# A four-direction scan block in fp32: all four directions of an image in one step of eight lines, ordered by a list scheduler

## The chip, the core and the metric

The kernel runs on one core of a Trainium2 chip; everything is fp32. The metric is the device time of one launch in microseconds (us), the median of several. The core's engines run side by side, each through its own queue in order: TensorE (PE; its weight loads are listed as PEld), VectorE (DVE), ScalarE (ACT), GpSimd (POOL) and SyncE (SP), which here issues the transfers (DMAs). Where an engine needs another's result, its instruction waits at the head of its queue.

## What is computed

The input is x[4, 128, 96, 96]. It is group-normalised, read as four sequences of 9216 positions per image (row by row, the same backwards, column by column, the same backwards), each sequence goes through the block below, and the four results are put back in place, mixed by a 1x1 convolution and added to x:

```python
t = grouped1x1(x, in_proj_w, in_proj_b, 4); u, gate = t[:, :256], t[:, 256:]
u = conv5_depthwise(silu(u), dw_w)
s = ssm_in_w @ u                                  # 32 channels
a = 0.999 + 0.0009 * sigmoid(ssm_delta_w @ u + .) # decay of the scan
bb, cc = tanh(ssm_b_w @ u + .), tanh(ssm_c_w @ u + .)
h[n] = a[n] * h[n-1] + bb[n] * s[n]               # along the sequence
u = u + ssm_out_w @ (cc * h + ssm_d * s)
y = out_proj_w @ grouped1x1(u * sigmoid(gate), mix_w, mix_b, 4) + .
out = x + fuse_w @ concat(y of the four directions)
```

The 256 channels of u stand in two halves of 128 partitions, j = 0 and j = 1. mix, out_proj and fuse are folded into one weight, w_fin, per direction.

## The kernel before

**Tiling.** An image is done in two phases, first the two vertical directions, then the two horizontal ones; the eight phases make up the launch. A phase has six steps of 16 lines. The positions of a step are kept by their residue modulo 4 (R = 4, order of the residues 1, 0, 3, 2), 384 positions each. One pair n (192 in all, 24 a phase) is one residue of one step for both directions, s = 0 and s = 1; the backward direction works from the other end of the image. So in the first three steps of a phase (here: fresh pairs) both directions meet new lines, and their silu tiles and gates are computed and also stored to DRAM; in the last three (mirrored pairs) each meets the lines that the other has had, and silu tiles and gates come back from DRAM, read backwards.

**A pair, with the names of the order table.** `F0..F3`/`SIL` (L245, L647): input projection and silu, fresh only; sixteen 32x32 products. `C0, C1` (L245, tile `band`): most of the convolution of half j = 0 as products with band matrices of 128 rows; the taps that reach over the band's edge come by `L` (tile `less`, 64-row products, for two residues of four) or by `E` (L766, one DVE operation on a tile `edge` that a DMA has shifted over the partitions). `T0` (L783, ACT) and `T1..T4` (L785, DVE): the five taps of half j = 1. `P0a..P1b` (L245, `u,main`): projections to delta, b, s, c, 32 rows for each direction, so s, b and the scan stand on 64 partitions. `TM, SC, CT` (L801, L809, L812), `SS` (L830), `DEC, BS` (L823, L826, POOL): the scan's inputs. `SCAN0, SCAN1` (L843, DVE): once for four residues, in two halves of 64 partitions x 768. `CH, ADD, CP` (L849, L853, L856, POOL). `UND` (L862, ACT copies u into PSUM), `S` (L866, ssm_out added there), `G`/`TH` (L872, L878: gate, fresh only), `GAT` (L919, DVE). `W` (L245, `u,w_fin`): four products of 32 columns each for a direction and half. `YS` (L932, L930) and `ACC` (L972, POOL): added to `acc`, the whole image in SBUF. While an image is done, the group statistics of the next are taken from chunks of it (`XC` loads 128x768 into `xs`, two `BN_STATS`, L518).

**Order.** Five tables are written out: `PLAN` (the operations of a pair's slot for four kinds of slot), `LAGS` (how many pairs an operation lags), `BANKS`, `START` and `END` (first eight slots and last six, operation by operation). PSUM has eight banks, handed out by `rent`. Every transfer takes one of eight semaphores in turn, so an issue also waits until the transfer eight places before it has landed; in the built program these are DMAHW0 to DMAHW7, in both kernels.

All small products are issued through one helper (L245), so its line stands for F, C, L, P and W; they are told apart by their tiles:

```python
def mm(o, col, lhsT, rhs, start, stop):      # L243
    r = slice(32 * col, 32 * col + 32)
    nc.tensor.matmul(o[r, : rhs.shape[-1]], lhsT, rhs, start=start, stop=stop,
                     skip_group_check=True)
def conv_less(n, to):                        # L, for two residues of four
    for g in range(4):
        for s in range(2):
            r = less_rows(s, p)              # 64 rows
            mm(bank(to[s]), g, less[p][r, g, :], columns(step, sil[s][r, g, :], k), False, True)
def result(n, s, j, to):                     # W
    for c in range(4):
        mm(bank(to), c, w_fin[:, units[2 * n + s]["dir"], j, 32 * c : 32 * c + 32],
           us[n][:, s, j, :], first, not first)
```

An fp32 product shows as two records in the trace, so "x8" in a row of it is four products.

Of the kernel before, what the change touches and what calls it, by code (L numbers as in the profile page):

```python
# [1 line left out]

# [40 lines left out]
F32 = mybir.dt.float32  # L43
# [14 lines left out]
LN = 16  # L58
NS = HH // LN
N = LN * WW // R  # L60
M = WW // R
UB = 8
NP = NS * R

PLAN = {
    "front": """
        T1 F1 F3 CP YS1 TM F2 F0 DEC P1b T2 P0b W01 AU0 SIL1 SIL3 SIL0 W00 SC BS T3 T4 SIL2 ZERO
        UND1 SCAN0 UND0 AU1 YS0 G00 C0 C1 S11 CT SS S00 ACC0 ACC1 S10 G01 SCAN1 S01 CH BN G10 E
        AFTER TH0 G11 L W10 W11 GAT0 TH1 UC P0a GAT1 ADD TH2 P1a T0 TH3
    """,  # L70
    "both": """
        YS1 T1 F2 F0 TM CP SCAN1 T2 F3 F1 C0 C1 SIL1 SIL0 P0b SIL2 T3 DEC SIL3 ZERO P1b L S11
        S10 T4 CT CH G10 SS G00 UC ADD TH2 W01 UND1 E AFTER W00 SC G01 ACC1 BN S01 YS0 ACC0 S00
        UND0 G11 AU1 TH0 GAT1 AU0 W10 W11 TH1 SCAN0 BS GAT0 P0a P1a T0 TH3
    """,
    "gate": """
        P0b YS1 CP AU1 P1b ACC1 T1 TM T2 AU0 UND1 C1 DEC CT C0 SC W00 L T3 SS T4 UND0 W01 BS S11
        E AFTER SCAN1 S10 G00 CH UC YS0 S00 G01 G11 TH0 BN S01 ACC0 G10 SCAN0 TH1 GAT1 W11 W10
        ADD P1a T0 P0a TH3 GAT0 TH2
    """,  # L80
    "none": """
        C0 T1 C1 TH1 P0b L W00 CP T2 P1b YS1 W01 TH0 TM ACC1 TH3 UND0 CH UC S01 E AFTER UND1 SC
        DEC T3 YS0 S00 G10 G11 AU0 S10 S11 T4 SCAN1 CT G01 BS BN G00 ADD SCAN0 GAT1 ACC0 AU1 TH2
        T0 P0a W10 SS W11 P1a GAT0
    """,
}
LAGS = {
# [6 lines left out]
}  # L94
BANKS = {
# [87 lines left out]
def conv_preact_kernel(  # L183
# [52 lines left out]
    def bank(i):  # L236
        return psum[:, i, :]
# [1065 lines left out]
```

## Time and profile before

| | before |
|---|---|
| median of two runs | 1777.9 us (1777.7 to 1778.11) |
| profiled execution: its span | 1770.6 us |
| instructions: PE, DVE, ACT, POOL | 22584, 1541, 2571, 1500 |
| mean granted TensorE clock | 0.994 (0.83 in the first 30 us, 0.93 from 30 to 100 us) |
| moved by DMA | 377.69 MB, 213 GB/s |
| launch to first input projection | 24.0 us |

The profile's first part gives each engine's busy time and its share of the span; products overlap on PE, so its busy share says only that something was in flight. A row of the groups has line, engine, operation, tiles, shape and count, then busy time, mean duration of one in ns, then the idle time ahead of it and what ended it. A row of the timeline has start and length in us. The median of the runs lies 7.3 us above the span of the profiled execution.

### The profile page before, as it was taken

Reading aid. Unit: us, or ns where it says so; the run is one execution under the profiler, and the core shown is the slowest. Engines: PE = TensorE matmul, PEld = TensorE weight load, DVE = VectorE, ACT = ScalarE, POOL = GpSimd, SP = SyncE. Lnnn points to the kernel's source line nnn. Section 1 sums busy time; section 2 is a strip of 40 time slices with the busy share of each in tenths; the row PEclk is TensorE's granted clock in tenths of the full one; section 3 lists DMA queues with packets and bytes.
Section 4 is the critical chain, followed back from the end, with each engine's and each line's share of the span. In section 5 each row is a group of like instructions: output and inputs, shape, how many; then the busy total and the mean of one; then the engine's idle time right before and its main releaser. Section 6 shows DMA issues by size and latency. Waiting matters only on the chain.

```text
span 1770.6 us, 54587 instructions
## 1 busy us (share of the span) xinstructions
PE 1747.7 (99%) x22584; PEld 638.7 (36%) x22584; DVE 1516.8 (86%) x1541; ACT 1486.1 (84%) x2571; POOL 1394.0 (79%) x1500
## 2 busy tenths in 40 slices
PE   6999999999999999999999999999999999999999
PEld 3333333333333333333333333333333333333333
DVE  4899988888788988988888988898888878888898
ACT  5788888888888888888888888888888888888875
POOL 4488888878778888788877888878777788887776
PEclk7999999999999999999999999999999999999999
DMA  7776676665987678564798657755589755656654
GB/s 229 180 238 232 180 227 187 201 204 175 295 261 235 209 209 241 182 204 165 218 293 264 231 188 227 223 179 198 165 257 278 250 193 181 209 159 198 215 190 165
DMA packets 183767, 377.69 MB, mean 213 GB/s; under 512 B 16736, under 2 KB 147040, under 8 KB 183520
## 3 DMA queue, kind: packets, MB, share of 16 engines
q1 hardware_dynamic: 183376, 374.16, 67.4%
q8 instruction: 178, 2.92, 0.7%
q14 instruction: 69, 0.57, 0.1%
q10 hardware_dynamic: 144, 0.04, 0.0%
HBM read 222.96 MB, written 151.18 MB: 211 GB/s over the span
## 4 chain that ended last, share of the span: by engine, by line
PE 91%; DMA 3%; ACT 2%; issue 1%; SPq 1%; DVE 1%; POOL 0%; ACTq 0%; POOLq 0%; DVEq 0%
PE psum L245 78%; PE psum L866 10%; PE psum L872 4%; DMA acc<-in_xr 2%; DMA out<-acc 1%; ACT gate L878 1%; POOL acc L972 0%; SPq L713 0%; DMA x_in<-in_xs 0%; ACT psum L862 0%; DVE u L919 0%; ACT sil L647 0%; DMA edge<-edge 0%; ACT u L748 0%; ACT t L812 0%
## 5 line engine op out<-in xcount | busy, mean ns | idle before, releaser
L785 DVE SCALAR_TENSOR_TENSOR psum<-sil,small,psum 128x768 f32<-128x768 f32 x576 | 588.1, 1022 | 56.1 <-ACT psum L783 38.1
L245 PE MATMUL psum<-u,w_fin 128*32 128x384 f32 x6144 | 580.0, 490 | 0.9
L245 PE MATMUL psum<-u,main 128*32 128x384 f32 x6144 | 562.2, 488 | 1.8 <-ACT gate L878 0.7
L972 POOL TENSOR_TENSOR acc<-ys,acc 128x384 f32<-128x384 f32 x365 | 422.1, 1165 | 155.2 <-ACT ys L932 76.8
L919 DVE SCALAR_TENSOR_TENSOR u<-gate,psum 128x768 f32<-128x768 f32 x376 | 346.0, 951 | 97.1 <-PE psum L866 69.9
L245 PEld LDWEIGHTS psum<-u,main 128*32 128x32 f32 x6144 | 186.6, 109 | 325.9 <-issue 216.0
L245 PEld LDWEIGHTS psum<-u,w_fin 128*32 128x32 f32 x6144 | 175.3, 109 | 342.8 <-issue 241.9
L862 ACT COPY psum<-u 128x768 f32<-128x768 f32 x352 | 278.1, 800 | 23.6 <-DVE u L766 8.4
L849 POOL TENSOR_TENSOR t<-t,t 64x384 f32<-64x384 f32 x192 | 235.1, 1225 | 68.4 <-DVE t L843 32.2
L245 PE MATMUL psum<-sil,band 128*32 128x384 f32 x3072 | 287.6, 490 | 1.1 <-ACT ys L932 1.1
L866 PE MATMUL psum<-t,main 32*128 32x384 f32 x1536 | 257.4, 530 | 1.3 <-ACT psum L862 1.3
L853 POOL TENSOR_TENSOR t<-t,t 64x384 f32<-64x384 f32 x192 | 236.9, 1234 | 7.6
L878 ACT ACTIVATE gate<-psum,bnorm 128x384 f32<-128x384 f32 x384 | 211.7, 577 | 33.4 <-PE psum L872 15.6
L826 POOL TENSOR_TENSOR t<-t,tm 64x384 f32<-64x384 f32 x191 | 196.0, 1026 | 51.1 <-ACT t L809 39.0
L823 POOL TENSOR_SCALAR t<-tm 64x384 f32<-64x384 f32 x191 | 179.7, 941 | 51.3 <-ACT tm L801 36.2
L647 ACT ACTIVATE sil<-psum,bnorm 128x385 f32<-128x385 f32 x384 | 200.4, 581 | 22.4 <-PE psum L245 21.8
L785 DVE SCALAR_TENSOR_TENSOR u<-sil,small,psum 128x768 f32<-128x768 f32 x192 | 194.7, 1014 | 18.2
L783 ACT ACTIVATE psum<-sil,small 128x768 f32<-128x768 f32 x192 | 173.7, 905 | 36.2 <-DVE u L919 31.5
L872 PE MATMUL psum<-x_in,wn 32*128 32x384 f32 x768 | 187.9, 516 | 0.2
L801 ACT ACTIVATE tm<-psum,small 128x384 f32<-128x384 f32 x192 | 112.5, 586 | 59.5 <-PE psum L245 57.2
L245 PEld LDWEIGHTS psum<-sil,band 128*32 128x32 f32 x3072 | 97.2, 110 | 152.4 <-issue 102.1
L932 ACT COPY ys<-psum 128x384 f32<-128x384 f32 x278 | 133.1, 479 | 21.3 <-POOL acc L972 10.9
(84 smaller groups left out, 1442.3 us busy)
## 6 DMA issues: line engine op xcount, KB each, us to landing
sil<-sil SPq DMA_DIRECT2D x128, 770.0 KB, 7.1
kept<-gate SPq DMA_DIRECT2D x80, 768.0 KB, 4.4
gate<-kept SPq DMA_DIRECT2D x76, 768.0 KB, 5.7
edge<-edge SPq DMA_DIRECT2D x96, 384.0 KB, 5.9
x_in<-in_xs SPq DMA_DIRECT2D x192, 96.2 KB, 3.5
edge<-sil SPq DMA_DIRECT2D x96, 192.5 KB, 3.9
acc<-in_xr SPq DMA_DIRECT2D x47, 384.0 KB, 7.8
out<-acc SPq DMA_DIRECT2D x44, 384.0 KB, 3.8
```

Of the source, the lines that this page charges most:

```text
L245: nc.tensor.matmul(o[r, : rhs.shape[-1]], lhsT, rhs, start=start, stop=stop, skip_group_check=True)
L647: nc.scalar.activation(sils[step][:, j, s, g, :], bank(frm)[:, : N + 1], AF.Silu, bias=bn[:, 1:2] if j else bn[:, 4 + g : 5 + g],)
L785: nc.vector.scalar_tensor_tensor(u_of(n)[:, :, 1, :] if k == K - 1 else part, src, w_tap[:, k : k + 1], part, ALU.mult, ALU.add,)
L826: engine.tensor_mul(scan_of(n)[0:64, pair_of(n)["p"], :], tbs[n][0:64, :], tms[n][0:64, :])
L849: engine.tensor_mul(ta[0:64, p, :], tbs[n][64:P, :], ta[64:P, p, :])
L853: engine.tensor_add(z, scans[n // R][0:64, pair_of(n)["p"], :], z)
L862: nc.scalar.copy(two(to), us[n][:, s])
L866: nc.tensor.matmul(bank(to)[:, :N], w_so[r, bass.ts(j, P)], tbs[n][r, :], start=not seeded(n), stop=True, skip_group_check=True)
L872: nc.tensor.matmul(bank(to)[:, :N], stats[pair_of(n)["b"]][0][r, s, :], x_in[s][r, q, off : off + N], start=True, stop=True)
L878: nc.scalar.activation(gates[n % 2][:, s, j, :], bank(frm)[:, :N], AF.Tanh, bias=bn[:, 2 + j : 3 + j], scale=0.5,)
L919: nc.vector.scalar_tensor_tensor(v, g, 1.0, two(frm), ALU.add, ALU.mult)
L972: nc.gpsimd.tensor_add(to, y, part)
```

## The change

The kernel is written anew around another split of the same work.

- **Split.** The four directions of an image are done together. A step has eight lines (12 steps an image, 6 fresh and 6 mirrored), a residue has 192 positions in each direction, and one n (192 in all) is one residue for four directions; operations that took 2 x 384 columns take 4 x 192. Projections to delta, b, s, c are done for two n at once (`P`, 384 columns, four directions on 4 x 32 partitions), so `DEC`, `BS`, `SS`, `CH`, `ADD` take 128 partitions and are half as many, and `SCAN` is one operation of 128 x 768 for a step. `CP` and the ACT copy `UC` are gone.
- **Edges.** `L` is gone. The taps that the band does not cover come from the tile `edge`: residues 0 and 3 need one, residues 1 and 2 need two. Fresh: `E` for one, `EH` and `E` for two, all DVE. Mirrored, two taps: `ES` (ACT) and `EA`, `EB` (POOL, 128 x 768) make `pre`, and DVE adds it (`E`). The edge tile is filled by 32 transfers of 32 x 386 a fresh step (SBUF to SBUF) and 8 of 128 x 386 a mirrored one (from DRAM).
- **Results.** `W` runs 192 columns at a time, for two directions into one bank: eight products where there were four. `YS` covers two directions, `ACC` adds each by itself, 128 x 192, in pieces of 8 or of 2 adjoining columns.
- **Statistics.** `XC` loads one chunk of 128 x 384, into one buffer `xs`; 72 of them for 72 `BN_STATS`.
- **Order.** No tables: every operation is added to a `Plan` with its reads and writes, a cost and a rank, and a list scheduler goes through assumed time and gives each free engine its ready operation of lowest rank. It takes a transfer to land 2 us after its bytes have gone through at 330 GB/s, and knows nothing of the eight semaphores.

```diff
-LN = 16
+S4 = 4
+BL = 8
...
-PLAN = { ... }  LAGS = { ... }  BANKS = { ... }  END = """ ... """  START = """ ... """
+COST = {"F": 890, "G": 860, "S": 860, "C": 645, "PJ": 645, "W": 645, "turn": 113, ... "T": 1022, "GAT": 951, "SCAN": 2100, "ACC": 650, ... }
+RANK = {"F": -4.33, "SIL": 0.47, ... "BN": -1.47, "STAT": 0.44}
+                if e == "SP":
+                    dma_free = max(dma_free, now) + pick.bytes / 330.0
+                    heapq.heappush(events, (now + 60, tick, 0, pick))
+                    tick += 1
+                    heapq.heappush(events, (dma_free + 2000, tick, 1, pick))
...
-    def conv_less(n, to): ...
+                if fresh:
+                    for g in range(R):
+                        dma(f"LE{k0}_{e}_{h}_{i}_{g}", k0 + 2 * e - 1.2, ...
+                                to[32 * g : 32 * g + 32],
+                                sil[32 * blk : 32 * blk + 32, ti, 0, g, 2 * h : 2 * h + 2, :]), ...)
...
+            nc.vector.tensor_tensor_scan(
+                t, t, bsb.rearrange("p n r -> p (n r)"),
+                0.0 if st == 0 else hbuf[:, 1 - hs, N - 1, R - 1 : R], ALU.mult, ALU.add)
...
+                    for o in range(2):
+                        s = 2 * h + o
+                        for c in range(4):
+                            mm(bank(w[key][0])[:, o * N : o * N + N], c,
+                               w_fin[:, DIRS[s], j, 32 * c : 32 * c + 32], ubuf[:, j, s, sl, :],
+                               j == 0 and o == 0, j == 1 and o == 1)
...
+    def chunk(b, c, n):
+        dma(f"XC{b}_{c}", n - 1.5, lambda: nc.sync.dma_start(xs, xr[b, :, bass.ds(c * SC, SC)]),
+            P * SC * 4, reads=[("done", n - 3)], writes=["xs"])
+        add(f"BN{b}_{c}", "DVE", "BN", n + RANK["BN"],
+            lambda w: nc.vector.bn_stats(stats_of(b)[:, c, :], xs), reads=["xs"], writes=[("bn", b, c)])
...
-        start()
-        for t in range(HEAD, NPAIR - TAIL):
-            slot(t)
-        tail()
+        for _, op, w in seq:
```

Where instructions stand now, at three places. On PE in the fresh half, before (L866 is `S`, L872 is `G`, `band` is C, `less` is L):

```order
L866 MATMUL psum<-t_56_5947,main 128x384 x2
L872 MATMUL psum<-x_in_70,wn_4136 128x384
L866 MATMUL psum<-t_56_5947,main 128x384
L872 MATMUL psum<-x_in_70,wn_4136 128x384
L872 MATMUL psum<-x_in_71,wn_4136 128x384
L866 MATMUL psum<-t_56_5947,main 128x384
L872 MATMUL psum<-x_in_71,wn_4136 128x384
L245 MATMUL psum<-u_5763,w_fin 32x384 x8
L245 MATMUL psum<-u_6417,main 32x384 x16
L245 MATMUL psum<-sil_5425,band 32x384 x8
L245 MATMUL psum<-u_5868,w_fin 32x384 x4
L245 MATMUL psum<-sil_5425,less 32x384 x8
```

and now (L855 is `S`, L633 `G`, `x_f` F):

```order
L250 MATMUL psum<-u,main 32x384 x4
L250 MATMUL psum<-u,w_fin 32x192 x8
L855 MATMUL psum<-csb,main 128x384 x4
L250 MATMUL psum<-u,w_fin 32x192 x48
L855 MATMUL psum<-csb,main 128x384 x4
L250 MATMUL psum<-sil,band 32x2x192 x8
L633 MATMUL psum<-x_g,wn_323 128x384 x4
L250 MATMUL psum<-x_f,wn_323 32x386 x16
L250 MATMUL psum<-u,main 32x384 x20
```

The 64-row products are gone, `S` and `G` stand in sets of four products and no longer mixed, and `W` has twice the products. Counted over the whole order, runs of 128-row products (`C`, `P`, `W` between others) go from 357 to 329.

On DVE in a fresh step now (L725 is `E`, L741 `T`, L815 `SCAN`, L957 `BN_STATS`):

```order
L725 SCALAR_TENSOR_TENSOR u<-edge,small,psum 128x4x192
L741 SCALAR_TENSOR_TENSOR psum<-sil,small,psum 128x4x192 x2
L957 BN_STATS bn_682<-xs 128x6
L741 SCALAR_TENSOR_TENSOR psum<-sil,small,psum 128x4x192
L741 SCALAR_TENSOR_TENSOR u<-sil,small,psum 128x4x192
L725 SCALAR_TENSOR_TENSOR u<-edge,small,psum 128x4x192
L815 SCALAR_TENSOR_TENSOR h<-h,bs 128x768
L741 SCALAR_TENSOR_TENSOR psum<-sil,small,psum 128x4x192
L957 BN_STATS bn_682<-xs 128x6
```

A chunk's load is released by the `E` of three n before it (or by the chunk before, if that is later), and its `BN_STATS` stands close behind: in 38 of the 72 cases at most three operations lie between.

On SP in a fresh step now (L591 and L598 fill `edge`, L954 is the chunk's load, L660 stores gates, L557 the silu tile, L509 and L623 load x):

```order
L660 DMA gate_5_0_280<-gate 128x1536
L660 DMA gate_5_1_281<-gate 128x1536
L954 DMA xs<-in_xr 128x384
L591 DMA edge<-sil 32x386 x16
L954 DMA xs<-in_xr 128x384
L623 DMA x_g<-in_xg 128x768
L954 DMA xs<-in_xr 128x384
L591 DMA edge<-sil 32x386 x4
```

A fresh step now issues 51 transfers (32 edges, 8 silu, 4 gates, 4 chunks, 3 of x), and the launch 1724 where it issued 1037; several chunk loads stand right behind 8 to 16 edge loads.

More of the change, by code (lines that the diff above doesn't have):

```diff
@@ L388, in load @@
+        return one, two, three, four, five, six, seven, eight, nine
     def load(src, name, pool=wp, queue=nc.scalar):
@@ L487, in conv_preact_kernel @@
     nc.scalar.activation(b_fin, pb[:, 0:1], AF.Identity, bias=b_fuse)
+    nc.vector.tensor_scalar_mul(b_fin, b_fin, 0.5)
     prep.__exit__(None, None, None)
[L490 to L509 removed]
@@ L598, in conv_preact_kernel, with buf @@
-    opened = set()
-    def opens(key):
-        opened.add(key) if (first := key not in opened) else None
-        return first
-    sils, edges, us, scans, tbs, tms, yss, old_gates = {}, {}, {}, {}, {}, {}, {}, {}
-    qb, qc, qa, qs = (slice(MH * i, MH * (i + 1)) for i in range(4))
+    wk = ctx.enter_context(tc.tile_pool(name="work", bufs=1))
+    def buf(name, *shape):
+        return wk.tile([P, *shape], F32, tag=name, name=name)
+    sil = buf("sil", 2, 2, R, S4, N + 1)
+    ubuf = buf("u", 2, S4, UB, N)
```

1624 lines of the change are left out of this document (748 added, 876 removed), and 15 rows, old and new, of tables (COST, LAGS, MOVES).

## Prediction

> **What bounds the kernel now.** First the page: its shares, then the chain of waits.
>
> ```profile
> span 1770.6 us, 54587 instructions
> PE 1747.7 (99%) x22584; PEld 638.7 (36%) x22584; DVE 1516.8 (86%) x1541; ACT 1486.1 (84%) x2571; POOL 1394.0 (79%) x1500
> PE 91%; DMA 3%; ACT 2%; issue 1%; SPq 1%; DVE 1%; POOL 0%; ACTq 0%; POOLq 0%; DVEq 0%
> ```
>
> PE is in flight for 99% and carries 91% of the chain. Overlapping products make that share a poor measure of work, so next the timeline of PE, whose start-to-start distances are the price of each kind of set:
>
> ```profile
> 265.12 0.88 PE L245 MATMUL psum<-sil,less 64*32 64x384 f32 x16
> 265.93 1.50 PE L245 MATMUL psum<-u,w_fin 128*32 128x384 f32 x16
> 268.64 0.95 PE L245 MATMUL psum<-x_in,wn 32*32 32x385 f32 x32
> 269.52 1.50 PE L245 MATMUL psum<-u,main 128*32 128x384 f32 x16
> ...
> 609.76 0.59 PE L866 MATMUL psum<-t,main 32*128 32x384 f32 x2
> ...
> 611.58 1.50 PE L245 MATMUL psum<-u,w_fin 128*32 128x384 f32 x16
> ...
> 615.47 0.83 PE L245 MATMUL psum<-u,main 128*32 128x384 f32 x8
> 616.12 0.83 PE L245 MATMUL psum<-u,w_fin 128*32 128x384 f32 x8
> 616.76 0.83 PE L245 MATMUL psum<-u,main 128*32 128x384 f32 x8
> 617.41 0.83 PE L245 MATMUL psum<-u,w_fin 128*32 128x384 f32 x8
> 618.16 0.93 PE L866 MATMUL psum<-t,main 32*128 32x384 f32 x8
> 619.02 0.85 PE L245 MATMUL psum<-u,main 128*32 128x384 f32 x8
> ```
>
> Four 128-row products (x8) step by 0.645 us. The stretch from 611.58 to 618.16 has ten such sets: 6.58 - 6.45 = 0.13 us for leaving the shape. Four S products cost 0.86, the sixteen of F 0.88, the eight 64-row ones 0.81. Before, the order holds 1920 sets of 128-row products in 357 runs, 96 L, 96 F and 288 S or G sets: 1238 + 46 + 78 + 84 + 248 = 1694. The other 77 of 1770.6 us are the start, the slower clock there, the end, and waits. So the order is tight and PE's work sets the time; DVE is next.
>
> **The change part by part**, against the 1770.6 us of the profiled execution (the median is 7.3 above).
>
> *PE.* L goes: 96 x 0.81 = -78. 357 runs become 329: 28 x 0.13 = -4. Mixed S and G go: between 609.76 and 611.58 eight of them took 1.82 (62 such runs average 1.87, this is one); two sets of four are 2 x 0.86 = 1.72: 62 x 0.15 = -9. P, C, F, G, S and W keep their columns. New floor: 1238 + 43 + 84 + 248 = 1613.
>
> *W in pieces of 192 columns* has 6144 more records, each with a weight load:
>
> ```profile
> L245 PEld LDWEIGHTS psum<-u,w_fin 128*32 128x32 f32 x6144 | 175.3, 109 | 342.8 <-issue 241.9
> ```
>
> 175.3 / 6144 is 28.5 ns a load. Four loads, 114 ns, must pass while a half-length record set of 0.645 / 4 = 161 ns streams; before, they passed under 322 unseen. I take 0; bounds 0 and 6144 x 28.5 ns = +175. The Trainium skill ("TensorE: Matmul & The Clock Gate", Part 3, The mechanism) says that a weight load overlaps running products only when its row group differs. All W products use all rows, so by that rule nothing would hide and the kernel would lose those 175 us. The rows disagree already: by the rule eight loads would lengthen each 0.645 us set, yet 16 or 8 records scale without any remainder.
>
> *DVE, ACT, POOL.*
>
> ```profile
> L785 DVE SCALAR_TENSOR_TENSOR psum<-sil,small,psum 128x768 f32<-128x768 f32 x576 | 588.1, 1022 | 56.1 <-ACT psum L783 38.1
> L919 DVE SCALAR_TENSOR_TENSOR u<-gate,psum 128x768 f32<-128x768 f32 x376 | 346.0, 951 | 97.1 <-PE psum L866 69.9
> L766 DVE SCALAR_TENSOR_TENSOR u<-edge,small,psum 128x768 f32<-128x768 f32 x96 | 97.0, 1011 | 16.7 <-PE psum L245 13.2 <-DMA edge<-edge 2.6
> L843 DVE TENSOR_TENSOR_SCAN t<-t 64x768 f32<-64x768 f32 x56 | 112.4, 2007 | 8.0 <-POOL t L826 4.8 <-POOL t L823 1.6
> L518 DVE BATCH_NORM_STATS2 bn<-xs 128x6 f32<-128x384 f32 x72 | 36.4, 548 | 0.0
> L972 POOL TENSOR_TENSOR acc<-ys,acc 128x384 f32<-128x384 f32 x365 | 422.1, 1165 | 155.2 <-ACT ys L932 76.8 <-ACT ys L930 63.4 <-DMA acc<-in_xr 3.0
> L853 POOL TENSOR_TENSOR t<-t,t 64x384 f32<-64x384 f32 x192 | 236.9, 1234 | 7.6
> L748 ACT COPY u<-psum 128x768 f32<-128x768 f32 x96 | 76.7, 799 | 32.1 <-PE psum L245 23.5 <-DVE psum L785 4.1 <-DVE bnorm L354 2.8
> L830 ACT ACTIVATE t<-t,small 64x384 f32<-64x384 f32 x192 | 118.2, 616 | 4.3
> ```
>
> A step of DVE now: 16 taps x 1.02 and 8 GAT x 0.95 as ever; one scan, 2.0, where there were two halves (48 for 96, about -100 us in all); E: 6 x 1.01 in a fresh step, 4 in a mirrored one (240 for 96, +145); 4 BN_STATS x 0.55 in most fresh ones. That is 16.4 + 7.6 + 2.0 + 6.1 + 2.2 = 34.3 fresh and 30.0 mirrored. PE, with 40 sets, 4 S and four runs: 25.8 + 3.4 + 0.5 = 29.7 mirrored; fresh, with 4 G and 4 F more and about ten runs, 25.8 + 6.9 + 3.5 + 1.3 = 37.5. So in the fresh half PE keeps the lead; in the mirrored half DVE comes level and sets 30.0: 24 x 0.2 to 0.3, say +4 (PE's runs are rounded down here). Before, four mirrored pairs cost PE 25.8 + 3.4 + 2 x 0.81 + 0.9 = 31.7 and DVE 16.4 + 7.6 + 2.0 + 4.0 = 30.0, so DVE could be 1.7 us late without harm. Now neither can wait for the other unpaid. I add 0.75 us of waits a step, 24 x 0.75 = +18; bounds 0, and 2 us (a little more than the slack that is gone), +48. ACT loses L748's 77 us and half of L830's 118, and gets 48 ES of some 0.9: it falls and bounds nothing. POOL's mirrored step: 16 ACC of half the size (0.58 is half of L972's mean, 0.71 leaves a fixed share), 8 operations of 384 columns at no more than L853's 1.23, two EA and two EB of twice that length at no more than 2.46: at most 29 to 31. I take it as under DVE; at the dear end it stands 1 us above, 24 us, inside the +48.
>
> *Chunk loads.* The scheduler's landing time is 2.0 + 0.6 us; in the trace:
>
> ```profile
> DMA packets 183767, 377.69 MB, mean 213 GB/s; under 512 B 16736, under 2 KB 147040, under 8 KB 183520
> ...
> xs<-in_xr SPq DMA_DIRECT2D x36, 384.0 KB, 3.8
> x_in<-in_xs SPq DMA_DIRECT2D x192, 96.2 KB, 3.5
> edge<-edge SPq DMA_DIRECT2D x96, 384.0 KB, 5.9
> edge<-sil SPq DMA_DIRECT2D x96, 192.5 KB, 3.9
> SPq L759 <- DMA edge<-edge: 81.8, 24, 5.2
> ```
>
> 192 KB lie between 3.5 and 3.8, say 3.65. By the order, the work on DVE between a load's release and its BN_STATS is at most 2.0 us in 27 cases, 3.1 in 11: 27 x 1.65 + 11 x 0.55 = 51 us in which DVE stands still and all its taps and GATs with it. Eighteen fresh steps have chunks, and DVE's slack there is 18 x (37.5 - 34.3) = 58. Cover in total, though not at the right moment: I take +15 (bounds 0 and 51).
>
> *Start and end.*
>
> ```profile
> 24.01 9.07 PE L245 MATMUL psum<-x_in,wn 32*32 32x385 f32 x128 [0.28 <-DVE bnorm L354]
> 35.49 5.65 DVE L785 SCALAR_TENSOR_TENSOR psum<-sil,small,psum 128x768 f32<-128x768 f32 x6 [11.33 <-ACT psum L783]
> 1700.00:1771.00 71.00, 66.92 (x796) 23.28 (x784) 60.47 (x69) 44.68 (x70) 45.67 (x45) 1.00 0.52 184
> ```
>
> Before, the first 64 products of F took 9 us, four at a time; sixteen together cost 0.88, so -5 and as much again in the next set. Against that, PE has 34 us of work in its order before the first S, while DVE has 20 taps and 8 E, 29 us, to do from about 34 before the first scan, and CH and ADD follow on POOL: the first S comes near 70, and PE stands idle for some 9 of those 46 us. Net 0 (bounds -9 and +9). At the end PE was in flight for 66.9 of the last 71 us. Now POOL has 24 ACC, two CH and two ADD behind the last scan, 24 x 0.65 + 4 x 1.2 = 20 us, and the last store, against 15 us of PE work and the end as it was: +8 (bounds 0, 15).
>
> *Sum.* 1770.6 - 78 - 4 - 9 + 0 + 4 + 18 + 15 + 0 + 8 = 1725 span, plus 7: **1732 us**, 2.6% below 1777.9. All unknowns at their good ends: 1725 - 18 - 15 - 9 - 8 + 7 = 1682; at their bad ends, W left out: 1725 + 30 + 36 + 9 + 7 + 7 = 1814.
>
> **The rivals.**
>
> *DVE becomes the bound.* Edge loads stand ahead of chunk loads on SP, so a chunk lands a microsecond later still: 27 x 2.65 + 11 x 1.55 + 7 x 0.75 = 94, 36 above the cover of 58, so 21 more than taken, and mirrored waits 1.65 us a step, 22 more: 1775, no difference. For: L518 waited 0.0 only because a load of two chunks came a pair ahead. Against: PE's queue holds other work.
>
> *The eight landings on SP set the fresh step (slower).* An issue waits for the transfer eight back; L759's wait for its own earlier edge, 81.8 us, is such a row. 51 transfers at 3.9 us are 51 x 3.9 / 8 = 25 us of 37.5, hidden. From a mean landing of 5.9 us it decides, and edge<-edge already has that. More bytes speak for it: about 437 MB by the shapes, for 377.69. At 6.5 us a fresh step is 41.4: 24 x 3.9 = +94, 1826 us. Against: most are 48 KB edges.
>
> *The loads of W show (slower).* From the point where four loads outlast 161 ns PE pays for them; all of them make 1732 + 175 = 1907. For: no product set in this trace is so short. Against: 47 ns of room.
>
> *All waits are covered.* PE's floor with the old start and end: 1725 - 18 - 15 - 8 + 7 = 1691. For: the order before lost next to nothing (PE in flight for all but 4 us of the last 71). Against: it was level with no other engine.
>
> **How the numbers follow.** The forecast 0.50 (own range 1695 to 1755), all covered 0.08, DVE bound 0.26, SP 0.11, W 0.05. A measurement tells about 2% from no change: below 1742 or above 1813. Of the forecast's 0.50 some 0.42 lie below 1742. Faster 0.42 + 0.08 = 0.50, same 0.08 + 0.26 = 0.34, slower 0.16. The range 1685 to 1814 runs from a little above the good ends to the bad ends; it leaves out W, most of SP and the outer edges of the others.
>
> **What would show it.** Right: no L rows; 192-column W sets of eight products in 0.65 us; S sets at 0.86; DVE near 1530 us busy (1517 + 145 - 100 and some 30 less for an operation that only the first pairs had), ACT below 1400; BN_STATS with idle time of some 50 us ahead of them, ended by the load; mirrored steps near 31 us, fresh ones near 38. Wrong: PE busy but W sets of 0.8 us (loads show), SP waiting for DMAs in most of a fresh step, or mirrored steps of 34 us with DVE waiting on POOL.

## The result, and the profile after

| | median us | ratio to the kernel before, 95% interval |
|---|---|---|
| before | 1777.9 (1777.7 to 1778.1, 2 runs) | 1 |
| changed | 2137.7 (2131.6 to 2143.9, 2 runs) | 1.2021 (1.1937 to 1.2104) |

The change makes the kernel 20% slower, where 1732 us were forecast, with 1685 to 1814 as the range: 406 us above the forecast. The page of the changed kernel, the same lines as before, with the clock:

```profile
span 2142.3 us, 63464 instructions
PE 1807.1 (84%) x27192; PEld 820.6 (38%) x27192; DVE 1489.3 (70%) x1586; ACT 1265.8 (59%) x1894; POOL 1119.9 (52%) x1375
PEclk8689999999998999999988899999998999999998
PE 42%; DMA 17%; DVE 17%; ACT 7%; SPq 6%; POOL 5%; issue 5%; DVEq 0%; POOLq 0%; ACTq 0%
```

The work has fallen on DVE, ACT and POOL, as it should, and PE's 1807 us are hardly more than before. But no engine carries the chain: PE has 42% of it where it had 91%, and DMA and SP's queue together have 23%. A chain that changes hands so often says that the engines wait for each other. What they wait for stands behind the bar in the groups:

```profile
L741 DVE SCALAR_TENSOR_TENSOR psum<-sil,small,psum 128x768 f32<-128x768 f32 x576 | 586.8, 1019 | 168.9 <-ACT psum L739 159.2
L868 DVE SCALAR_TENSOR_TENSOR u<-gate,psum 128x768 f32<-128x768 f32 x384 | 349.0, 948 | 163.1 <-PE psum L855 130.5
L957 DVE BATCH_NORM_STATS2 bn<-xs 128x6 f32<-128x384 f32 x72 | 40.2, 559 | 178.2 <-DMA xs<-in_xr 178.0
L918 POOL TENSOR_TENSOR acc<-ys,acc 128x192 f32<-128x192 f32 x768 | 526.1, 700 | 412.3 <-ACT ys L901 263.3
```

The durations (1019, 948, 559, 700 ns) are the forecast's. What it lacks is idle time: DVE alone stands 178 us before BN_STATS for a chunk's load and 159 us before a tap for ACT's first tap.

The length of each step follows from the starts of the 48 scans (L815) in DVE's timeline, of which these are the first and the last:

```profile
103.16 1.74 DVE L815 TENSOR_TENSOR_SCAN h<-h,bs 128x768 f32<-128x768 f32 x1
...
2107.51 1.82 DVE L815 TENSOR_TENSOR_SCAN h<-h,bs 128x768 f32<-128x768 f32 x1 [5.08 <-POOL bs L804]
```

| mean us | forecast | changed | e5 | e8 | e9 | e13 | e14 |
|---|---|---|---|---|---|---|---|
| start to the first scan | 67 | 103.2 | 90.5 | 83.0 | 84.9 | 83.9 | 85.0 |
| 15 fresh steps with chunks | 38 | 48.4 | 42.1 | 43.7 | 47.8 | 45.3 | 41.9 |
| 5 fresh steps, last image | 38 | 44.2 | 40.8 | 41.5 | 45.2 | 44.0 | 41.1 |
| 4 first mirrored steps | 31 | 39.5 | 39.9 | 39.2 | 39.6 | 41.6 | 39.6 |
| 20 further mirrored steps | 31 | 37.1 | 36.4 | 36.0 | 38.9 | 32.9 | 33.4 |
| 3 turns to the next image | 38 | 52.1 | 41.0 | 46.4 | 47.9 | 44.3 | 44.6 |
| last scan to the end | | 34.8 | 35.0 | 34.7 | 34.7 | 33.5 | 32.4 |

(A step is the distance from one scan to the next; e5 to e14 are runs told below.) Nothing is lost in one place: 36 us at the start, 15 x 10.4 + 5 x 6.2 = 187 in fresh steps, 4 x 8.5 + 20 x 6.1 = 156 in mirrored ones, 3 x 14 at the turns.

Two theories came out of this trace. **Banks**: S, F and G take four PSUM banks at once, where the kernel before took two for S and one at a time for F and G (its `rent`), and T holds two through five operations; so PSUM would be full too often, and the order would have to wait for banks. Its rows are waits that no data can explain. F and G read x and weights, yet PE stands before them until DVE has done, which frees their banks:

```profile
L250 PE MATMUL psum<-x_f,wn 32*32 32x386 f32 x3072 | 102.2, 539 | 65.4 <-DVE u L725 38.0 <-DMA x_f<-in_xf 12.3 <-ACT gate L646 7.6
L633 PE MATMUL psum<-x_g,wn 32*128 32x384 f32 x768 | 106.9, 544 | 34.3 <-DVE u L741 14.8 <-DVE u L725 10.4 <-DVE u L868 4.5
```

**Late transfers**: chunk loads, and at the turns acc's loads, come later than the order assumes. Of what makes them late there was no theory yet. The rivals: the turns by themselves; PE's clock, which the page shows at 0.8 and 0.9 wherever PE idles.

### The profile page after: what moved, and what is told of

It is laid out like the page before. It is cut to its first block, busy times and chain, and to the rows that moved or that the text cites. A ratio compares the mean times of both kernels' runs of the same rounds, so it can differ in the third digit from the quotient of the medians.

```text
span 2142.3 us, 63464 instructions
## 1 busy us (share of the span) xinstructions
PE 1807.1 (84%) x27192; PEld 820.6 (38%) x27192; DVE 1489.3 (70%) x1586; ACT 1265.8 (59%) x1894; POOL 1119.9 (52%) x1375
## 4 chain that ended last, share of the span: by engine, by line
PE 42%; DMA 17%; DVE 17%; ACT 7%; SPq 6%; POOL 5%; issue 5%; DVEq 0%; POOLq 0%; ACTq 0%
PE psum L250 34%; DMA xs<-in_xr 7%; DVE psum L741 6%; PE psum L855 5%; DVE u L868 5%; SPq L591 4%; DMA edge<-sil 3%; PE psum L633 3%; DMA gate<-gate 3%; POOL acc L918 2%; DVE u L725 2%; ACT gate L646 2%; DVE u L741 2%; ACT sil L534 1%; DMA sil<-sil 1%
## 5 line engine op out<-in xcount | busy, mean ns | idle before, releaser
L918 POOL TENSOR_TENSOR acc<-ys,acc 128x192 f32<-128x192 f32 x768 | 526.1, 700 | 412.3 <-ACT ys L901 263.3
L741 DVE SCALAR_TENSOR_TENSOR psum<-sil,small,psum 128x768 f32<-128x768 f32 x576 | 586.8, 1019 | 168.9 <-ACT psum L739 159.2
L250 PE MATMUL psum<-u,w_fin 128*32 128x192 f32 x12288 | 576.9, 333 | 33.6 <-DVE u L868 21.7
L250 PEld LDWEIGHTS psum<-u,w_fin 128*32 128x32 f32 x12288 | 385.6, 112 | 274.9 <-issue 82.9
L646 ACT ACTIVATE gate<-psum,bnorm 128x768 f32<-128x768 f32 x192 | 164.2, 899 | 147.4 <-PE psum L633 126.2
L855 PE MATMUL psum<-csb,main 32*128 32x384 f32 x1536 | 229.1, 556 | 17.7 <-ACT psum L846 15.8
L534 ACT ACTIVATE sil<-psum,bnorm 128x772 f32<-128x772 f32 x192 | 163.5, 903 | 65.7 <-PE psum L250 64.2
L741 DVE SCALAR_TENSOR_TENSOR u<-sil,small,psum 128x768 f32<-128x768 f32 x192 | 194.6, 1014 | 6.1
L901 ACT ACTIVATE ys<-psum,b_fin 128x384 f32<-128x384 f32 x192 | 111.4, 580 | 138.7 <-PE psum L250 128.2
L698 POOL TENSOR_SCALAR pre<-edge,small 128x768 f32<-128x768 f32 x48 | 105.9, 2206 | 118.2 <-DVE u L722 77.6
L957 DVE BATCH_NORM_STATS2 bn<-xs 128x6 f32<-128x384 f32 x72 | 40.2, 559 | 178.2 <-DMA xs<-in_xr 178.0
L725 DVE SCALAR_TENSOR_TENSOR u<-edge,small,psum 128x768 f32<-128x768 f32 x144 | 145.5, 1011 | 25.4 <-PE psum L250 20.3
L830 POOL TENSOR_TENSOR csb<-csb,h 128x384 f32<-128x384 f32 x96 | 117.3, 1234 | 77.3 <-DVE h L815 73.1
```

What stands on the lines that cost most here:

```text
L250: nc.tensor.matmul(o[r], lhsT, rhs, start=start, stop=stop, skip_group_check=True)
L534: nc.scalar.activation(t[:, j, g].rearrange("p (h o) n -> p h (o n)", h=2), psum[:, w0 : w0 + 2, : 2 * (N + 1)], AF.Silu, bias=bn[:, 1:2] ...
L646: nc.scalar.activation(gate[:, ring[j], :, i].rearrange("p (h o) n -> p h o n", h=2), psum[:, w0 : w0 + 2, : 2 * N].rearrange("p h (o n) - ...
L725: nc.vector.scalar_tensor_tensor(to, views[-1], w_edge[:, k : k + 1], pc, ALU.mult, ALU.add)
L741: nc.vector.scalar_tensor_tensor(ubuf[:, 1, :, slot] if k == K - 1 else part, src, w_tap[:, k : k + 1], part, ALU.mult, ALU.add)
L830: add(f"CH{n0}", "POOL", "CH", step_end + RANK["CH"] + late, lambda w: nc.gpsimd.tensor_mul(z, z, hv), reads=[("h", hs, d)], writes=[("csb ...
```

## The experiments

All times below are medians of four runs beside the kernel before on the same chip (1776.4 to 1780.4 us), except e12. "The scheduler's account" is the end of the order by the scheduler's own constants (its table of durations, 2.0 us a landing, 0.06 us an issue, eight banks): 1987 us for the part of the change that it orders. It is arithmetic of the kernel's own, and no chip time.

### e1: S in pairs of directions

```diff
-                    takes=[] if h else [(x, 2, "SS", True) for x in keys])
+                    takes=[(keys[h], 2, "SS", True)])
...
-                for s in range(S4):
...
+                    for o in range(2):
+                        s = 2 * h + o
```

> The S sets (the state's products onto u) are cut in two: two directions, two PSUM banks at a time, each pair with its own UND before and GAT behind; the scheduler orders the whole anew with the same ranks. By the theory that the order is bound by PSUM (four banks at once for S, F and G, where the kernel before took two) the mirrored steps fall from 33-35 us to 31-33 and the time by about the 58 us that the scheduler's own account gives (1987 to 1929): 2040 to 2100 us for 2138. Two S products alone may cost PE more than half of a set of four (0.43 us is assumed); if they cost 0.65, 192 x 0.4 = 77 us come back where PE is the last to be ready. By the theory that late chunk loads and the image turns make up the loss, the time stays within 2120 to 2150, since neither is touched.

Measured: 2211.2 us, ratio 1.2401 (1.2316 to 1.2487): 73 us slower, not 58 faster. PE's timeline shows the price that the expectation allowed for. First the change, where four products are 8 records, then e1, where two are 4:

```profile
838.89 0.93 PE L855 MATMUL psum<-csb,main 32*128 32x384 f32 x8
839.75 1.50 PE L250 MATMUL psum<-u,main 128*32 128x384 f32 x16
```

```profile
720.50 0.91 PE L856 MATMUL psum<-csb,main 32*128 32x384 f32 x4 [0.71 <-ACT psum L846]
721.35 1.51 PE L250 MATMUL psum<-u,w_fin 128*32 128x192 f32 x32
```

From its start to the start of what follows, a pair takes 0.85 us and a set of four 0.86: as long. So 192 x 0.86 = 165 us of PE came in with the banks, and the run says nothing of the banks alone. (A set of four runs its products side by side in four row groups. The Trainium skill, "TensorEngine Tiling (Array Packing)", section "Gotcha 1: PSUM Pressure", says that different row tiles write to different PSUM banks; by that the four-bank set cannot be made smaller by shorter products. No run here tried it.)

### e2: chunks loaded ahead

```diff
-        dma(f"XC{b}_{c}", n - 1.5, lambda: nc.sync.dma_start(xs, xr[b, :, bass.ts(c, SC)]),
...
+        def fetch():
+            for x in range(3) if c == 0 else [c + 2] if c < 18 else [c] if c >= 20 else []:
+                nc.sync.dma_start(to(x), xr[b, :, bass.ts(x, SC)])
...
```

> Order of all operations unchanged; 20 of an image's 24 chunk loads have three buffers in turn (xs and two halves of the buffer pre, which is not in use then), and each place in the order loads the chunk two further on, so that BN_STATS finds its chunk landed. By the theory that late chunk loads make up the loss, the 178 us that BN_STATS waits fall below 50 and the time by 100 us or more, to 2040 or less. By the theory that PSUM banks bind the order, the wait falls just as far but most of it comes back as waits of DVE and PE for one another: 30 to 60 us less, 2080 to 2110.

Measured: 2090.0 us, ratio 1.1738 (1.1705 to 1.1772): 48 us less. The wait before BN_STATS falls as expected:

```profile
L964 DVE BATCH_NORM_STATS2 bn<-pre 128x6 f32<-128x384 f32 x39 | 21.6, 554 | 4.0 <-DMA pre<-in_xr 4.0
L964 DVE BATCH_NORM_STATS2 bn<-xs 128x6 f32<-128x384 f32 x33 | 18.3, 556 | 37.6 <-DMA xs<-in_xr 37.6
```

178 - 42 = 136 us of waiting less gave 48 us less time; the rest came back as other waits. Late chunks are a part, and not the whole.

### e3: the turn's loads left out

```diff
-                    lambda a=a, c=c: nc.sync.dma_start(
+                    lambda a=a, c=c: None if st == NST - 1 else nc.sync.dma_start(
```

> Order unchanged; the loads that bring x of the next image into the outermost ring of blocks of acc (behind the last step of an image, three turns) are left out, so that the outer ring of images 1 to 3 lacks its x. POOL's wait for them, 79 us in three pieces, goes to nearly none. If the turns are waited for by everything, the time falls by 50 to 80 us, to 2060 to 2090; if other work of the turn covers them (the first F and its silus have no need of acc), by less than 20.

Measured: 2118.4 us, ratio 1.1899 (1.1873 to 1.1925): 19 us less, and the three turns hardly shorter (51.5 us on the mean for 52.1). Other work covers these loads; this theory falls.

### e4: S, F and G in halves, taps in SBUF

```diff
-                part = spread(w0)
+                part = ubuf[:, 1, :, slot]
...
-                takes=[] if k else [(tkey, 2, "T", False)],
-                frees=[(tkey, "T")] if k == K - 1 else [])
+                )
```

> S, F and G are cut in two (two banks at a time), and the five taps of T accumulate in their place in u in SBUF, so that T takes no PSUM bank; ordered anew with the same ranks. The scheduler's account gives 1882 for 1987. By the theory of the banks the time falls by about as much, 105 us, to 2000 to 2060. By the rivals (chunk loads, turns, PE's slower clock) it stays above 2110. DVE's taps that now write SBUF should take 1.0 us as before.

Measured: 2439.1 us, ratio 1.3691 (1.3661 to 1.3722): 301 us slower. All of S, F and G now pay e1's price, and a second one is new. Two groups of e4, DVE's taps and POOL's sums into acc:

```profile
L742 DVE SCALAR_TENSOR_TENSOR u<-sil,small,u 128x768 f32<-128x768 f32 x768 | 978.3, 1278 | 123.1 <-ACT u L740 111.4
...
L917 POOL TENSOR_TENSOR acc<-ys,acc 128x192 f32<-128x192 f32 x768 | 745.3, 981 | 465.7 <-ACT ys L900 360.7 <-ACT ys L898 82.8 <-DMA acc<-in_xr 3.9
```

With its second input in SBUF and not in PSUM a tap takes 1278 ns for 1019 on the mean, and POOL's sum, whose code is the same, 981 ns for 700. Sorted by what runs beside them in e4's trace, the 147 taps with POOL idle have a median of 1.01 us and the 350 with POOL busy throughout 1.35; the 303 sums without a tap beside them have 0.69, those with a tap beside them for more than half of their time 1.37 to 1.39. So it is the two engines' meeting that costs, not SBUF by itself. My expectation of 1.0 us was wrong. (The Trainium skill, "SBUF — State Buffer", section "SBUF: two separate sides", says that a DVE operation with two SBUF inputs and a GpSimd operation that reads SBUF lock each other out; the two rows agree.) So in this kernel, whose POOL works beside them, taps belong in PSUM, and this run, too, leaves the theory of the banks open.

Reading on in the chain of the change, in order of time, one place stood out: a chunk's load that waits for nothing but its turn. The timeline of SP's queue there:

```profile
708.77 1.14 SPq L660 DMA_DIRECT2D gate<-gate  x2
710.00 1.14 SPq L954 DMA_DIRECT2D xs<-in_xr  x1
711.23 12.44 SPq L591 DMA_DIRECT2D edge<-sil  x16
723.78 0.53 SPq L954 DMA_DIRECT2D xs<-in_xr  x1
```

Sixteen edge loads hold SP for 12.4 us, 0.78 each on the mean of this block, before the chunk (L954) is issued at 723.78. DVE has to take the chunk next, and stands until it lands:

```profile
727.34 0.56 DVE L957 BATCH_NORM_STATS2 bn<-xs 128x6 f32<-128x384 f32 x1 [1.25 <-DMA xs<-in_xr]
```

An issue is not free. The scheduler counts 0.06 us for it. That is theory **Q**: SP's queue is an engine of its own, with 51 issues of 0.63 (the steady step of this block, and e12's) to 0.78 us in a fresh step, an estimate of 32 to 40 us of work, and the order does not know it.

### e5: three of four edge loads left out

```diff
-                            lambda to=to, blk=blk, g=g, h=h: nc.sync.dma_start(
+                            lambda to=to, blk=blk, g=g, h=h: None if g and k0 else nc.sync.dma_start(
```

> Order unchanged; from the second step on, three of every four of the 48 KB edge loads of a fresh step are not issued (24 of 32; the rows of edge that they would fill keep old values). Theory Q (new, after the runs before): SP's queue of transfers is what the order overlooks. In the profile of the change an edge load holds SP for 0.78 us (503 us in 647 seen issues), where the scheduler counts 0.06, so a block of 16 holds chunk, gate and silu transfers behind it for 10 to 12 us. By it the time falls by 90 to 130 us, to 2010 to 2050, though no work of PE, DVE, ACT or POOL is left out. By the theory of PSUM banks, and by that of PE's slower clock after idle time, the transfers matter only through the chunks, and what e2 gained (48 us) is about all: 2085 to 2110.

Measured: 1968.0 us, ratio 1.1046 (1.1019 to 1.1072): 170 us less, more than expected, with every compute instruction and its order the same. The chunks' wait is now

```profile
DVE bn L957 <- DMA xs<-in_xr: 33.7, 23, 4.7
```

for 178.0 us in 49 times. In the table of steps, 95 of the 170 us come from fresh steps with chunks, 33 from the turns, 17 from the last image's fresh steps, 13 from the start: everywhere that edges are loaded in small pieces, and where acc's loads stand in the queue behind them.

### e6: the scheduler told 0.6 us

```diff
-        op = plan.add(name, "SP", 60, rank, act, size=size, **kw)
+        op = plan.add(name, "SP", 600, rank, act, size=size, **kw)
```

> The same program, but the scheduler counts 0.6 us of SP for each transfer in place of 0.06, and orders everything anew. Its own account rises from 1987 to 2010. Theory Q: an order that knows the price loses less by it, 30 to 60 us less, 2080 to 2110. If SP's issues don't matter, the order is as good as its own account, some 20 us slower: 2140 to 2170.

Measured: 2115.5 us, ratio 1.1884 (1.1862 to 1.1905): 22 us less, short of the 30 to 60 that Q gave, but not slower, as the account had it. Knowing the price helps little while the issues remain.

### e7 and e8: edges from the kept copy

```diff
-                if fresh:
-                    for g in range(R):
-                        dma(f"LE{k0}_{e}_{h}_{i}_{g}", k0 + 2 * e - 1.2,
...
+                src = kept_sil[b % 2][st if fresh else NST - 1 - st][0][blk]
+                dma(f"LE{k0}_{e}_{h}_{i}", k0 + 2 * e - (1.2 if fresh else 2),
+                    lambda to=to, src=src, h=h: nc.sync.dma_start(
+                        to, src.rearrange("g h s n -> (g h) s n")[:, 2 * h : 2 * h + 2, :]),
```

The stores to the kept copy get the rank k0 - 1.3 for k0 + 0.5. e8 has k0 - 3 there, k0 + 2 * e - 2 for the loads, and e6's line too.

> Fresh edges are loaded as the mirrored ones are: 8 loads of 193 KB a step from the copy of the silu tile that is kept in HBM, in place of 32 of 48 KB from SBUF (576 transfers less in all); the stores to that copy are ranked earlier. All results stay those of the reference. The scheduler still counts 0.06 us; its own account is 2005 for 1987, a little worse. Theory Q: 24 x 0.7 = 17 us of SP less in each of 24 fresh steps; the time falls by 70 to 110 us, to 2030 to 2070. If the order or the banks set the time, it stays within 2120 to 2160.

> Both: edges in 8 loads a step from the kept copy, issued somewhat earlier, and the scheduler counts 0.6 us a transfer. Theory Q: 100 to 140 us less than the change, 2000 to 2040. What is then left above the 1725 to 1732 that was predicted (some 290 us) cannot be SP's: it would be the order's own, whose account by the scheduler is 1999 here.

Measured: e7 2013.4 us, ratio 1.1324 (1.1283 to 1.1365), 124 us less; e8 1996.1 us, ratio 1.1222 (1.1185 to 1.1258), 142 us less, both a little more than expected. Q is shown by a kernel that leaves nothing out, against an account that rose. The edge loads in the change and in e8, count and the shortest, median and longest time that one holds SP, in ns:

```profile
L591 SPq DMA_DIRECT2D edge<-sil x768: 507/589/2177, 30.2 to 1847.7; - x192
```

```profile
L590 SPq DMA_DIRECT2D edge<-sil x384: 319/430/2936, 50.0 to 1905.0; - x192
```

e8's 384 are fresh and mirrored together, each four times the size. What is left is 1996 - 1732 = 264 us.

### e9: W with a bank too many

```diff
-                    takes=[] if j else [(key, 1, "W", False)], mode="N", full=[(key, True)])
+                    takes=[] if j else [(key, 2, "W", False)], mode="N", full=[(key, True)])
...
-CAPS = {"T": 8, "C": 3, "P": 5, "SS": 6, "W": 2, "F": 7, "G": 4, "X": 6}
+CAPS = {"T": 8, "C": 3, "P": 5, "SS": 6, "W": 4, "F": 7, "G": 4, "X": 6}
```

> As e8 (edges from the kept copy, the scheduler counts 0.6 us a transfer), but each half result W is given two PSUM banks where it fills one; the second stays empty. No instruction is added or lengthened on any engine; only the order, made anew, has to do with less PSUM (some 1180 more of 12,500 bank-us, 147 us over eight banks). If PSUM sets the time of what is left after the transfers, the kernel is 100 to 180 us slower than e8's 1996: 2100 to 2180. If the list order has banks to spare, it stays within 1980 to 2020.

Measured: 2144.2 us, ratio 1.2055 (1.2001 to 1.211): 148 us slower than e8, though no engine has anything more to do. W held 1180 bank-us, and now twice that: 1180 / 8 = 147 us. In this order a bank that is held and not used is paid for in full; whether a bank that is given back pays as much is tried in e13. It shows in the sums into acc, whose W comes later (238.3 us in e8's waits), and not in every wait (S is waited for 122.3 us here and 133.9 in e8):

```profile
POOL acc L909 <- ACT ys L892: 383.9, 104, 12.1
```

### e10 and e11: other ranks

e10 has e8's program with the numbers of RANK and CAPS (that set the order of ready operations) changed throughout; e11 the same with S in pairs as in e1.

> As e8, with other rank numbers and caps, chosen so that the same list of operations, played back with durations read from these profiles, ends earlier (21 us earlier than e8's in that playback). If what is left is due to badly chosen ranks, some other numbers should gain 50 us or more; if the banks and the four-bank sets bind, no choice of numbers gains much: 1965 to 1990.

> As e10, but with S cut in two (two directions and two banks at a time) and the scheduler told that such a pair takes 0.85 us of PE, as e1's profile shows; ranks chosen anew in the same way. PE then has up to 192 x 0.85 = 163 us more of S. If PSUM is dearer than PE, it still comes out level with e10 or up to 40 us below; if PE's time and clock decide, it is 30 to 100 us above e10.

Measured: e10 1996.7 us, ratio 1.1234 (1.12 to 1.1267), the same as e8 and above both expectations; e11 2017.7 us, ratio 1.1365 (1.1345 to 1.1384), 21 us above e10, between the two theories: of the 165 us more of PE only 21 show. Whether the banks that came free gave the rest back or PE's idle time took it in, the run does not tell. The numbers chosen for e10 did not gain their 21 us on the chip. That some other set of numbers gains more is not excluded, only that these did.

### e12: an issue by itself

```diff
+            if rows == 32:
+                queue.dma_start(dst[32 * g : 32 * g + 32, x], t(slice(32 * (x // 4), 32 * (x // 4) + 32), x))
+            else:
+                queue.dma_start(dst[:, x], t(slice(0, P), x))
```

> Nothing of the reference is computed (the output is zeros): five blocks of 16 transfers, each block by itself with every engine else quiet: from SP, SBUF to SBUF 32 rows of 1544 bytes (48 KB, as a fresh edge load); SBUF to SBUF 128 rows (193 KB); HBM to SBUF 32 rows; HBM to SBUF 128 rows (as e7's edge load); and from ACT's queue, SBUF to SBUF 32 rows. If an issue itself costs SP 0.6 to 0.8 us, the 16 small ones take 10 to 12 us from the first on; if the price is the wait for the transfer eight back, the first eight go at 0.1 us each and only the rest are slow. If the price belongs to the size, the 193 KB ones cost four times as much; if to the issue, about the same.

One run. The timeline of SP's queue, and of ACT's (L270 has 32 rows, L272 128; src lies in SBUF, held in HBM):

```profile
35.98 10.11 SPq L270 DMA_DIRECT2D dst<-src  x16
50.34 10.29 SPq L272 DMA_DIRECT2D dst<-src  x16
64.70 7.30 SPq L270 DMA_DIRECT2D dst<-held  x16
79.05 8.64 SPq L272 DMA_DIRECT2D dst<-held  x16
```

```profile
93.65 10.18 ACTq L270 DMA_DIRECT2D dst<-src  x16
```

On an idle chip an issue holds its queue for 0.63 us from SBUF, whether it moves 48 or 193 KB, and 0.46 to 0.54 us from HBM; on ACT's queue it is the same 0.64. The first eight go no faster, as the same block up to 41 us shows:

```profile
35.98 5.04 SPq L270 DMA_DIRECT2D dst<-src  x8
```

So it is not the wait for the transfer eight back: the small ones land in 1.9 us, and eight are issued in 5. The price belongs to the issue.

### e13 and e14: S's banks held for less, and no UND

```diff
-                    lambda w, us=us, key=keys[h]: nc.scalar.copy(view(w, key), us), banks=[keys[h]],
+                    lambda w, us=us: nc.scalar.copy(us, us),
...
-                    takes=[] if h else [(x, 2, "SS", True) for x in keys])
...
-                        z[r].rearrange("p i n -> p (i n)"), start=False, stop=True, skip_group_check=True)
+                        z[r].rearrange("p i n -> p (i n)"), start=True, stop=True, skip_group_check=True)
...
+                takes=[(x, 2, "SS", False) for x in keys], full=[(x, True) for x in keys], mode="R")
```

e14 drops the copy altogether.

> As e8, but UND copies u onto itself in SBUF and not into the PSUM banks of S; S starts its banks afresh and takes them only when it runs (so u is not added to S's sum, and the result lacks that term). ACT, PE and DVE do the same number of operations of the same size, and S still waits for UND. Only the banks of S are held for some 2 us less: 2168 bank-us for 3868 in the scheduler's account. If PSUM binds, the time falls: by the account 42 us, all of it in the mirrored steps (F and G, which also take four banks at once, use up what comes free in the fresh ones): 1940 to 1975, mirrored steps 1 to 3 us shorter. If something else binds, 1985 to 2010.

> As e13, with UND left out altogether (ACT has 384 copies of 0.8 us less, and S no longer waits for them). The account is 1866 for e8's 1999; the same order as e8's with UND at no cost would gain only some 50 us by the shorter chain. If PSUM binds, 1850 to 1890; if only the chain counts, 1930 to 1960; if neither, ACT being idle a third of the time, 1985 to 2010.

Measured: e13 1976.8 us, ratio 1.1108 (1.1076 to 1.1141), 19 us less than e8; e14 1910.4 us, ratio 1.0725 (1.0684 to 1.0766), 86 us less. e13 lands 2 us outside what the banks' theory gave. By the account S holds 2168 bank-us where it held 3868; the 1700 less are 212 us over eight banks, and gave 19, so bank time does not come back at the rate at which e9 paid for it. The table of steps shows why it is so little: the 20 mirrored steps fall by 3.1 us each, 62 us, and the fresh and the first mirrored ones rise by 1.6 to 2.5, 46 us. That the banks that S leaves free go to F and G, which take four at once as well and are then ahead of S, is argued and was not tried by itself. The waits for the first tap and for S fall. In e13, for 153.3 and 133.9 us in e8:

```profile
L732 DVE SCALAR_TENSOR_TENSOR psum<-sil,small,psum 128x768 f32<-128x768 f32 x576 | 587.0, 1019 | 116.5 <-ACT psum L730 95.4 <-PE psum L250 9.6
L859 DVE SCALAR_TENSOR_TENSOR u<-gate,psum 128x768 f32<-128x768 f32 x384 | 348.9, 949 | 134.1 <-PE psum L845 122.7 <-issue 3.7 <-DMA gate<-gate 1.8
```

Banks are not all that e13 changes. The order still has S behind UND, but on the chip S no longer waits for it. The products of S in e8 (UND is L837) and in e13:

```profile
L846 PE MATMUL psum<-csb,main 32*128 32x384 f32 x1536 | 232.3, 553 | 19.9 <-ACT psum L837 16.2 <-POOL sil L551 2.5 <-POOL acc L909 1.1
```

```profile
L845 PE MATMUL psum<-csb,main 32*128 32x384 f32 x1536 | 227.9, 542 | 54.5 <-DVE u L859 19.1 <-DVE u L732 16.1 <-ACT sil L534 7.0
```

The 16.2 us of waiting for UND's copy are gone, and in its place S waits for the DVE and ACT operations that free banks. So the 19 us belong to banks held for less and a wait less, together.

e14 falls between the two expectations, 20 us above that of the banks and 20 below that of the chain alone. So of the 264 us some 20 were got back by holding S's banks for less (with that wait gone) and 86 by that and a shorter chain; the others stay.

## Why the prediction was wrong

**PE's sets and floor: right.** No L is left, and sets cost what the rows of before gave. Two neighbours of the changed kernel, eight W products of 192 columns as 16 records and four P products:

```profile
709.59 0.85 PE L250 MATMUL psum<-u,main 128*32 128x384 f32 x8 [0.35 <-ACT gate L646]
710.26 0.83 PE L250 MATMUL psum<-u,w_fin 128*32 128x192 f32 x16
710.91 0.83 PE L250 MATMUL psum<-u,main 128*32 128x384 f32 x8
711.55 0.83 PE L250 MATMUL psum<-u,w_fin 128*32 128x192 f32 x16
```

The starts step by 0.65 us through all four, so the weight loads of W stay hidden, as taken, and the rival "the loads of W show" is out. The Trainium skill's rule on weight loads ("TensorE: Matmul & The Clock Gate", Part 3, "The mechanism"), which the forecast weighed and set aside, would have given 175 us more of W; these rows do not agree with it. (The same section also lets a load go ahead into the background weight buffer, which the forecast did not weigh; these rows do not speak against that.)

**The other engines: right in size.** DVE 1489 us (some 1530 forecast), ACT 1266 (below 1400), POOL's sum 0.70 us (0.58 to 0.71).

**The end: right.** 34.8 us from the last scan, 24 before: 10 for 8.

**The chunk loads: mis-sized.** The term was +15, at most 51. BN_STATS waited 178 us, and taking most of that wait away gave 48 (e2). The working took the load's flight, 3.65 us, and left out its place in the queue, 12 us behind 16 edges.

**SP: the right queue, the wrong price.** The rival "the eight landings on SP" priced a fresh step's 51 transfers at 51 x 3.9 / 8 = 25 us and called them hidden. The price is 0.63 to 0.78 us of the queue for each: an estimated 32 to 40 us, about as long as the 38 of the step that it should hide in, so that whatever stands behind a block of edges comes late. The rows were in the trace of before, whose kept silu tiles hold SP for 0.575 us each:

```profile
L668 SPq DMA_DIRECT2D sil<-sil x64: 524/575/1907, 117.7 to 1677.8; - x64
```

No term counted what the change adds there: 1724 - 1037 = 687 issues, 687 x 0.59 = 405 us of one in-order queue (that this is also the size of the miss is chance; added up in the two traces, the issues' own durations go from 584 to 1106 us, some 520 more). Undoing 576 of them gave 124 to 142 us (e7, e8).

**"PE keeps the lead", "DVE comes level and sets 30.0": the step that failed.** The lengths of a step were sums of engine time, 37.5 and 30.0, and waits between engines were one term, +18, at most 48. Nowhere was PSUM counted, though the change gives S, F and G four banks at once. By the scheduler's account of e8's order the banks are held for 12,475 bank-us: S 3868, T 2488, C 1584, P 1203, W 1188, F 1119, G 1002 and 23 of the statistics. A step holds 12,475 / 48 = 260, and 260 / 8 = 32.5 us is what all eight banks need if none is ever empty. The forecast's mean step, (38 + 31) / 2 = 34.5, leaves little room: 32.5 is 94% of it, with sets that can begin only when four are free together. (The holding times are those of this order, its waits included; a tighter order would hold for less, so this is an estimate and no floor.) The steps came out at 48.4 us for 38 and 37.1 for 31. e9 shows that banks set a price: 147 us of bank time more, 148 us of time. The mirrored step is where the miss shows without SP: 36.0 us for 31 in e8, and 32.9 in e13.

**"DVE becomes the bound" and "all waits are covered": wrong**, both for that reason; DVE was busy for 70%.

**The start: wrong.** 103 us to the first scan, forecast as before's 67. Of the 36, 20 are SP's (e8: 83.0); 16 are not accounted for.

**What stays open.** Of the 406 us, 142 were got back by issuing less (170 in e5, which leaves loads out). The 264 left agree with the order's own account: e8's, which counts eight banks, the table of durations and 0.6 us an issue, ends at 1999, counted from its first operation some 27 us into the launch, and e8 takes 1996 in all. Of these 264, the runs show that banks set a price (e9) and that some 20 to 86 can be had around S, by holding its banks for less and by a shorter chain; how much of the rest is banks, how much the list's order, is argued and not shown. The scheduler's account says 1777 with sixteen banks for 1987 with eight, all else the same; no run here could try that. PE's clock is open, too. It follows idle time: a product behind a wait of 7 us runs at half speed, as the 24 records at 835.02, 3.9 us for some 1.95, while the sets of S behind them are back at 0.86.

```profile
835.02 3.94 PE L250 MATMUL psum<-u,main 128*32 128x384 f32 x24 [7.16 <-DVE u L741]
838.89 0.93 PE L855 MATMUL psum<-csb,main 32*128 32x384 f32 x8
```

The mean granted clock is 0.994 before, 0.940 in the change, 0.970 in e8, 0.918 in e1 and 0.879 in e4, so the versions that wait more also run at a lower clock: 0.06 x 2142 = 129 us of clock withheld in the change, 60 in e8. How much of that lies on the path was not tried by itself. (The Trainium skill, "TensorE: Matmul & The Clock Gate", section "What's actually happening", says that the array runs at half clock after about 3.4 us of idling and until as long of work; these rows agree.)

None of these versions beats the kernel before; the nearest that computes all of the reference is e8, 12% slower.

## What to carry to other kernels

Sums of engine time are a floor only for what they count. Before taking one as the time, write the same sum for each in-order queue (issues x the time that one holds the queue) and for PSUM (banks x the time that each tenant holds them, over eight); a sum that comes near the length of the step is a warning (here 32 to 40 us of 38 on SP, 32.5 of 34.5 for the banks), above all where a tenant needs several banks at once. And an order that a scheduler made rests on its constants: compare each (0.06 us an issue, 2.0 us a landing) with the trace first, and read the end that it computes for itself, which here stood at 1987 us.

## What the runs showed of the hardware

- An issue holds its queue for 0.63 to 0.64 us on an idle chip when it reads SBUF, on SP at 48 and 193 KB and on ACT at 48, and on SP for 0.46 (48 KB) to 0.54 us (193 KB) when it reads HBM (e12); in the kernel's block of 16 that is shown it was 0.78 on the mean. The Trainium skill, "DMA: Bandwidth & Descriptors", section "Anatomy of one DMA — SWDGE (gpsimd) path", gives about 50 ns for the sequencer's dispatch, for another path; on these two queues the measurement decides.
- Two 32-row products of 384 columns take as long as four in four row groups: 0.85 and 0.86 us (e1 and the change).
- DVE's three-operand operation on 768 elements takes 1278 ns for 1019 on the mean with both inputs in SBUF, and POOL's sum 981 for 700 (e4); beside an idle partner they take 1.01 and 0.69 us, beside a busy one 1.35 and 1.37 to 1.39.
